# Another order of VectorE's and GpSimd's side work around the matmuls of a two-layer graph network

## The chip, the cores and the metric

The kernel runs on one core of one Trainium2 chip. The metric is the device time in microseconds, shown as the median of three runs. A profile of one further execution comes with it. In views of the profile PE is TensorE's matmul, PEld its weight load, DVE is VectorE, ACT is ScalarE, POOL is GpSimd, and SP is the queue that issues most DMAs.

## The reference

There are 32 independent inputs `x[b]` of 512 nodes by 512 features, all in float32, and one 512 by 512 adjacency matrix for all of them.

```python
# layer 0: attention over the graph, 8 heads of 64
q, k, v = x @ Wq + bq, x @ Wk + bk, x @ Wv + bv
w = softmax(q k^T / 8 + where(adj == 0, -1e9, 0))
x = layernorm(x + w v)
# layer 1: graph convolution
norm_adj = adj * deg**-0.5 (rows) * deg**-0.5 (columns)
x = layernorm(x + norm_adj @ (x @ weight) + bias)
```

## The kernel before, in words

The kernel goes over `b` = 0 to 31 in one long unrolled program. Almost every instruction goes through the helper class `InOrder` (line 45, which is why most rows of the profile name that line): it pins compute instructions to the order in which the program writes them, engine by engine. So the order in the text is the order on each engine.

**A pass and its two shares.** For each `b` there is a `stretch` over the first two pairs of attention-head pairs (`one`), then a list of matmul groups, then a `stretch` over the other two pairs (`two`), and a second list of matmul groups. I call the first list, with what runs beside it, the first share and the second list the second share. A `stretch` computes `scores` (tile `sc`, 32 matmul records on PE; VectorE subtracts the mask into `e`, ScalarE takes the exponential), then lets GpSimd sum the numerators (`acc`), and multiplies with the values (`av`, 32 records on PE).

- First share of `b`: keys and queries of the next input, `b + 1` (14 groups, tiles `kq`).
- Second share of `b`: the first product of the graph convolution of input `b - 1` (four groups, `first`), the values of input `b + 1` (`v`, eleven steps v[0] to v[10]), and the second product of the convolution (seven groups, `second`).

**Seven products for eight.** Keys, queries, values and the convolution are block products with seven multiplications instead of eight (`seven`). They need sums and differences of blocks of x transposed: `turn` transposes x into `XT[0..3]` on VectorE (two calls, `turn0` and `turn1`), and `combine` forms `XT[4..6]` and a new `XT[2]` on GpSimd (four operations). The values take one level more: v[0] to v[6] are `LEAF` groups on quarters of blocks, v[7] is an addition on GpSimd (`spread_last`), v[8] to v[10] are the `OUTER` groups. Their further combinations (`QUARTERS`, in `XT[7..10]`) are formed by `quarters`, four GpSimd operations. A group writes a PSUM bank and is then put (ScalarE) or added (VectorE) into its output. Groups named by the same letter in the table accumulate in the same bank, so the next of them may not write before the earlier one's put or add has read it. All three `OUTER` groups have one letter.

**Steps.** `play(main, beside)` issues the matmul groups of `main` one after the other, and behind group number n whatever `beside[n]` lists. I call n a step. In the second share for b = 1 to 29 the steps are: 0 to 3 `first`, 4 to 9 the leaf groups v[0] to v[5], 10 second[0], 11 the last leaf group v[6], 12 v[7], 13 v[8], 14 second[1], 15 v[9], 16 second[2], 17 v[10], 18 to 21 second[3] to second[6]. For b = 30 second[0] comes behind v[7] instead; for b = 0 there are only the eleven steps of `v`.

**What runs beside them.** `fold` (VectorE: one transposition and one reduction) finishes the softmax's sums; `inverse` is one small matmul (`folded`) and five VectorE operations; `scale` multiplies a row of the attention output by the inverse sums; `add` adds x (GpSimd); `measure`, `root`, `norm`, `low` and `lift` are the layer normalisation in pieces (`root` partly and `lift` wholly on GpSimd, `norm` on ScalarE, `low` on VectorE with the output `lo`); `grow` rescales on ScalarE; `bias_values` adds the values' bias row `bv_r` to one of four node rows of `V`.

DMAs of the pass go through SP: the head outputs' rearrangement (`yT<-yb`), two parts of the x after next, `wqv` in turn with the queries' and the values' weights (`swap`), and the outputs.

Of the kernel before, what the change touches and what calls it, by code (L numbers as in the profile page):

```python
# [50 lines left out]
def unshifted(  # L51
# [16 lines left out]
    NT = N // P  # L68
# [5 lines left out]
    tensor, vector, scalar, gpsimd = (InOrder(tc, e) for e in (nc.tensor, nc.vector, nc.scalar, nc.gpsimd))  # L74
# [24 lines left out]
    def each(f, *args):  # L99
        return [lambda a=a: f(*a) if isinstance(a, tuple) else f(a) for a in args]  # L100
# [22 lines left out]
    def load_x(b, j):  # L123
        if j == 1:
            X[b, j] = NUM[:, 7].rearrange("p k (n t r) -> p (k n) t r", t=DT, r=32)
        else:
            X[b, j] = acts.tile([P, 8, DT, 32], F32, name="x", bufs=1)
        for q in range(4):
            nc.sync.dma_start(
                X[b, j][32 * q : 32 * (q + 1)],  # L130
                x[b, ts(j, HALF), ts(q, P)].rearrange("(k s) (t r) -> s k t r", s=32, r=32),
            )

    def turn(b, j):
        vector.transpose(
            XT[:, 2 * j : 2 * j + 2].rearrange("p i u (k s) -> p (i u) k s", s=32),
            X.pop((b, j)).rearrange("p k t r -> p t k r"),
        )
# [26 lines left out]
    def combine(b, at):  # L165
        to, a, c = PARTS[at]
        engine = gpsimd if b else vector
        engine.tensor_tensor(XT[:, to], XT[:, a], XT[:, c], ALU.subtract)
# [15 lines left out]
    def load_residual(b):  # L184
        if b < LAST - 1:
            t = acts.tile([P, NT, D], F32, name="xr", tag="zT", bufs=1)
        else:
            t = wk[:, 3:].rearrange("p k u o -> p k (u o)")
        R[b] = [t[:, i, :] for i in range(NT)]
        for i in range(NT):  # L190
            nc.sync.dma_start(R[b][i], x[b, ts(i, P), :])
# [67 lines left out]
    def swap(k):  # L259
        nc.sync.dma_start(wqv, stored[k])  # L260
# [253 lines left out]
    def stretch(b, gs, gap=()):  # L514
        banks("attention")
        for g in gs:
            scores(b, g)
        for g in gs:
            accumulate(b, g)
        banks("products")  # L520
        for g in gs:
            av = bank([P, N], "av")
            values(b, g, av)
            unload_values(b, g, av)
            if g == gs[0]:
                run(gap)

    def fold(b, g):
        a = ACC.pop((b, g))[0]
        if g == ORDER[0]:  # L530
            SM[b] = small.tile([P, H, N // 32], F32, name="folded")
        vector.transpose(a.rearrange("p k n -> p (k n)"), a.rearrange("p k n -> p (k n)"))
        vector.tensor_reduce(
            SM[b][:, 2 * g : 2 * g + 2].rearrange("p k t -> p (k t)"),
            a.rearrange("p k (t s) -> p (k t) s", s=32), AX.X, ALU.add,
        )
# [306 lines left out]
    for b in range(B):  # L843
        one, two = ORDER[:2], ORDER[2:]
        f[b], c[b] = finish(b), convolve(b)
        ahead, back = f.get(b - 1), c.get(b - 2)
        if 1 < b < LAST:
            load_residual(b - 1)
        if b + 2 < B:
            load_x(b + 2, 0)  # L850
        if b == LAST:
            load_residual(b)
        stretch(b, one, back["measure"][:3] if back else ())

        def folds(gs):
            return [[lambda g=g, b=b: fold(b, g)] for g in gs]

        def turns(b=b + 2):
            if b >= B:
                return [], [], []  # L860
            return [lambda: turn(b, 0)], [lambda: turn(b, 1)], [lambda k=k: combine(b, k) for k in range(4)] + [quarters]

        fold0, fold1 = folds(one) if b < LAST else ([], [])
        rest = back["measure"][3:] + back["root"] if back else []
        store = back["store"] if back else []
        if b < LAST:
            k0, k1 = keys_and_queries(b + 1, 0), keys_and_queries(b + 1, 1)
            main = [p for pair in zip(k0, k1) for p in pair]
            if b == 0:
                exact = each(compare, *range(NT))  # L870
                weights = each(lambda k: weigh_part(w1, gpsimd, k), *range(4))
                beside = {
                    1: fold0, 2: [degrees], 3: weights[:1], 4: fold1, 5: weights[1:2] + exact[:1], 6: exact[1:2],
                    7: weights[2:3], 8: exact[2:3], 9: weights[3:], 10: exact[3:],
                }
            else:
                measure, norm, low = ahead["measure"], ahead["norm"], ahead["low"]
                scale = ahead["inverse"] + ahead["scale"] if b == 1 else []
                beside = {
                    0: rest + scale + ahead["add"], 1: store[:1] + fold0, 2: store[1:2], 3: store[2:3] + fold1,  # L880
                    4: store[3:] + measure[:2], 5: measure[2:] + ahead["root"], 7: norm[:1] + ahead["judge"],
                    8: norm[1:2] + low[:1], 9: norm[2:3] + low[1:2], 10: norm[3:] + low[2:3],
                    11: low[3:] + ahead["lift"],
                }
            play(main, beside)
        else:
            e = f[b]
            conv = c[b - 1]
            play(conv["first"], {
                0: rest + store[:1] + conv["parts"][:0], 1: store[1:2] + ahead["judge"] + conv["parts"][:1],  # L890
                2: store[2:] + e["sums0"],
                3: conv["parts"][1:] + e["inverse0"] + ahead["grow"],
            })

        if b < LAST:
            swap(1)
        stretch(b, two, f[b]["pairs"][0] + f[b]["pairs"][1] if b == LAST else ())

        fold0, fold1 = folds(two) if b < LAST else ([], [])
        turn0, turn1, combined = turns()  # L900
        if b + 2 < B:
            load_x(b + 2, 1)
        if b < LAST:
            end = f[b]
            v, bias_v = values_of(b + 1), each(bias_values, *((b + 1, n) for n in range(NT)))
            back_to_queries = [lambda: swap(0)] if b < LAST - 1 else []
            if b == 0:
                play(v, {
                    1: fold0, 4: fold1, 8: turn0, 9: turn1, 10: combined + back_to_queries + bias_v,
                })  # L910
            else:
                conv = c[b - 1]
                second = conv["second"]
                k = 6 if b < LAST - 1 else 8
                main = conv["first"] + v[:k] + second[:1] + v[k:9] + second[1:2] + v[9:10] + second[2:3] + v[10:] + second[3:]
                grow, parts, scale = ahead["grow"], conv["parts"], end["scale"]
                if b < LAST - 1:
                    bias_v = each(bias_values, *((b + 1, n, vector) for n in range(NT)))
                    beside = {
                        1: parts[:1] + fold0, 3: parts[1:], 5: fold1, 6: grow[:1], 8: grow[1:2], 9: grow[2:3] + end["inverse"],  # L920
                        10: grow[3:] + scale[:1], 11: scale[1:2], 13: turn0 + scale[2:3], 14: turn1 + scale[3:] + combined[:1],
                        15: combined[1:2], 17: combined[2:] + bias_v[:1] + back_to_queries, 18: bias_v[1:2],
                        19: bias_v[2:3], 20: bias_v[3:],
                    }
                else:
                    measure, norm, low = end["measure"], end["norm"], end["low"]
                    beside = {
                        0: [lambda: load_residual(LAST - 1)], 1: parts[:1] + fold0, 3: parts[1:], 5: fold1,
                        6: grow[:1], 8: grow[1:2], 9: end["inverse"], 10: grow[2:3] + scale[:2], 11: grow[3:] + scale[2:] + end["add"],
                        14: measure[:1], 15: measure[1:2], 16: measure[2:3],  # L930
                        17: measure[3:] + end["root"], 18: norm[:1] + bias_v, 19: norm[1:2] + low[:1], 20: norm[2:3] + low[1:2],
                        21: norm[3:] + low[2:] + end["lift"],
                    }
                play(main, beside)

# [5 lines left out]
    end, held, e = f[LAST], c[LAST - 1], c[LAST]  # L941
    pairs, halves, norm, low, block = (
        end["pairs"], end["halves"], end["norm"], end["low"], e["block"]
    )
# [302 lines left out]
```

## Time and profile before

| what | value |
|---|---|
| median of 3 runs | 2762.72 us (2760.16 to 2763.03) |
| profiled execution, own time | 2760.92 us |
| its span, first to last instruction | 2759.1 us |
| PE busy | 2715.4 us |
| VectorE busy | 2075.0 us |
| GpSimd busy | 1910.7 us |
| ScalarE busy | 1259.6 us |
| mean granted TensorE clock | 0.997 |

The page counts busy time of each engine over the whole span; the timeline gives the same instructions one by one; the waits say how long an engine idled and which engine's instruction ended that. From about 230 us on, one pass takes 84.47 us and repeats to the hundredth.

### The profile page before, as it was taken

Reading aid. Unit: us, or ns where it says so; the run is one execution under the profiler, and the core shown is the slowest. Engines: PE = TensorE matmul, PEld = TensorE weight load, DVE = VectorE, ACT = ScalarE, POOL = GpSimd, SP = SyncE. Lnnn points to the kernel's source line nnn. Section 1 sums busy time; section 2 is a strip of 40 time slices with the busy share of each in tenths; the row PEclk is TensorE's granted clock in tenths of the full one; section 3 lists DMA queues with packets and bytes.
Section 4 is the critical chain, followed back from the end, with each engine's and each line's share of the span. In section 5 each row is a group of like instructions: output and inputs, shape, how many; then the busy total and the mean of one; then the engine's idle time right before and its main releaser. Section 6 shows DMA issues by size and latency. Waiting matters only on the chain.

```text
span 2759.1 us, 36196 instructions
## 1 busy us (share of the span) xinstructions
PE 2715.4 (98%) x13284; PEld 1907.3 (69%) x13284; DVE 2075.0 (75%) x2925; ACT 1259.6 (46%) x1807; POOL 1910.7 (69%) x1219
## 2 busy tenths in 40 slices
PE   9899999999999999999999999999999999999997
PEld 6566776766767767667667676676676676766765
DVE  5777777778777777777787777777777877777777
ACT  3344444454434544444544445444445444454444
POOL 5667676676676676766766766767667677667675
PEclk9999999999999999999999999999999999999999
DMA  6223333333333233322333332333323333323321
GB/s 180 81 57 99 106 91 92 90 90 100 88 98 107 69 102 99 101 92 81 99 100 88 97 103 72 104 90 105 96 76 103 100 88 96 97 80 103 92 61 48
DMA packets 388185, 256.75 MB, mean 93 GB/s; under 512 B 278816, under 2 KB 346400, under 8 KB 379936
## 3 DMA queue, kind: packets, MB, share of 16 engines
q1 hardware_dynamic: 386848, 252.78, 30.5%
q8 instruction: 107, 1.75, 0.3%
q10 hardware_dynamic: 1152, 1.57, 0.2%
q14 instruction: 78, 0.64, 0.1%
HBM read 183.77 MB, written 37.22 MB: 80 GB/s over the span
## 4 chain that ended last, share of the span: by engine, by line
PE 90%; DVE 7%; issue 1%; POOL 1%; ACT 0%; DMA 0%; SPq 0%; DVEq 0%; POOLq 0%; ACTq 0%
PE mm L45 58%; PE av L45 16%; PE sc L45 16%; DVE xT L45 2%; DVE yT L45 2%; DVE v L45 2%; DVE y L45 1%; POOL xT L45 0%; DVE st L45 0%; DVE lo L45 0%; ACT yT L45 0%; ACT hi L45 0%; DVE e L45 0%; POOL y L45 0%; DMA xr<-in_x_dram 0%
## 5 line engine op out<-in xcount | busy, mean ns | idle before, releaser
L45 ACT ACTIVATE e<-e 128x1024 f32<-128x1024 f32 x512 | 541.4, 1057 | 614.8 <-DVE e L45 582.0
L45 DVE SCALAR_TENSOR_TENSOR e<-sc,maskT 128x1024 f32<-128x1024 f32 x512 | 584.8, 1213 | 103.1 <-PE sc L45 103.1
L45 POOL TENSOR_TENSOR acc<-acc,e 128x1024 f32<-128x1024 f32 x248 | 588.8, 2374 | 19.4
L45 POOL TENSOR_TENSOR xT<-xT 128x512 f32<-128x512 f32 x250 | 369.0, 1486 | 156.9 <-DVE xT L45 139.8
L45 PE MATMUL mm<-xT,wk 128*128 128x256 f32 x1792 | 463.5, 381 | 0.6 <-DVE kq L45 0.6
L45 PE MATMUL sc<-kq 64*128 64x512 f32 x2048 | 459.4, 597 | 1.8 <-DVE e L45 1.4
L45 PE MATMUL mm<-xT,wqv 128*128 128x256 f32 x1792 | 460.0, 379 | 0.0
L45 PE MATMUL av<-e,v 128*64 128x512 f32 x2048 | 455.4, 597 | 4.2 <-POOL v L45 4.0
L45 PEld LDWEIGHTS mm<-xT,wk 128*128 128x128 f32 x1792 | 337.3, 190 | 71.3 <-DVE mv L45 23.5
L45 POOL TENSOR_TENSOR acc<-e 128x1024 f32<-128x1024 f32 x126 | 297.3, 2360 | 118.5 <-ACT e L45 118.5
L45 PEld LDWEIGHTS mm<-xT,wqv 128*128 128x128 f32 x1792 | 340.4, 190 | 46.5 <-DVE wqv L45 0.2
L45 PEld LDWEIGHTS av<-e,v 128*64 128x64 f32 x2048 | 145.6, 137 | 306.6 <-issue 234.1
L45 PEld LDWEIGHTS sc<-kq 64*128 64x128 f32 x2048 | 191.7, 186 | 237.6 <-issue 182.6
L45 ACT ACTIVATE kq<-mm,bias 128x256 f32<-128x256 f32 x512 | 214.1, 472 | 295.7 <-PE mm L45 291.9
L45 PE MATMUL mm<-wqv,xT 128*128 128x128 f32 x1736 | 306.5, 322 | 15.2 <-DVE v L45 15.2
L45 POOL TENSOR_TENSOR yT<-yT,b_r 128x512 f32<-128x512 f32 x126 | 156.7, 1277 | 237.8 <-DVE lo L45 237.8
L45 DVE TENSOR_TENSOR v<-v,mm 128x512 f32<-128x512 f32 x221 | 148.6, 685 | 195.5 <-PE mm L45 195.3
L45 PEld LDWEIGHTS mm<-wqv,xT 128*128 128x128 f32 x1736 | 259.9, 191 | 49.3 <-DVE v L45 23.8
L45 DVE STREAM_TRANSPOSE yb<-av 128x512 f32<-128x512 f32 x127 | 91.0, 717 | 257.3 <-DMA yT<-yb 193.3
L45 PE MATMUL mm<-w,zT 128*128 128x256 f32 x992 | 229.5, 379 | 0.0
L45 PEld LDWEIGHTS mm<-w,zT 128*128 128x128 f32 x992 | 186.1, 190 | 24.8 <-issue 0.8
L45 PE MATMUL mm<-adjT,hi 128*128 128x512 f32 x512 | 201.6, 397 | 0.8 <-ACT e L45 0.8
(134 smaller groups left out, 3382.7 us busy)
## 6 DMA issues: line engine op xcount, KB each, us to landing
wqv<-wv_parts SPq DMA_DIRECT2D x31, 1792.0 KB, 7.5
wqv<-wq_parts SPq DMA_DIRECT2D x30, 1792.0 KB, 7.0
yT<-yb SPq DMA_DIRECT2D x508, 64.0 KB, 2.4
out_dram<-y SPq DMA_DIRECT2D x120, 256.0 KB, 2.0
xr<-in_x_dram SPq DMA_DIRECT2D x118, 256.0 KB, 3.3
x<-in_x_dram SPq DMA_DIRECT2D x124, 128.0 KB, 2.7
e<-in_x_dram SPq DMA_DIRECT2D x124, 128.0 KB, 2.6
wk<-in_x_dram SPq DMA_DIRECT2D x8, 256.0 KB, 2.7
```

What stands on the lines that cost most here:

```text
L45: return self.tc.keep_in_program_order(op(*args, **kwargs))
```

## The change

All of it lies in what stands beside the matmul groups.

- `quarters` for input `b + 2` are no longer formed behind `combine` in the second share of `b`, but in the first share of the next pass, behind `root` at step 5.
- In the second share, for b = 1 to 29: `inverse` moves from step 9 to step 7, `scale` from steps 10, 11, 13, 14 to 9, 10, 11, 14; the second transposition of x moves from step 14 to 15, and `combine` stands at steps 15 and 17. The bias of the values is added by GpSimd behind `combine` (four operations) and no longer by VectorE at steps 17 to 20.
- b = 0: `fold1` moves from step 4 to 5, and the bias comes behind two of the four `combine` operations.
- b = 30: `inverse` at step 7, the last row's `scale` at step 8, the others one step earlier, and everything behind them (`add`, `measure`, `root`, `norm`, `low`, `lift`) up to one step earlier.

```diff
-            return [lambda: turn(b, 0)], [lambda: turn(b, 1)], [lambda k=k: combine(b, k) for k in range(4)] + [quarters]
+            return [lambda: turn(b, 0)], [lambda: turn(b, 1)], [lambda k=k: combine(b, k) for k in range(4)]
...
-                    4: store[3:] + measure[:2], 5: measure[2:] + ahead["root"], 7: norm[:1] + ahead["judge"],
+                    4: store[3:] + measure[:2], 5: measure[2:] + ahead["root"] + [quarters], 7: norm[:1] + ahead["judge"],
...
-                    1: fold0, 4: fold1, 8: turn0, 9: turn1, 10: combined + back_to_queries + bias_v,
+                    1: fold0, 5: fold1, 8: turn0, 9: turn1 + combined[:2], 10: bias_v + combined[2:] + back_to_queries,
...
-                    bias_v = each(bias_values, *((b + 1, n, vector) for n in range(NT)))
                     beside = {
-                        1: parts[:1] + fold0, 3: parts[1:], 5: fold1, 6: grow[:1], 8: grow[1:2], 9: grow[2:3] + end["inverse"],
-                        10: grow[3:] + scale[:1], 11: scale[1:2], 13: turn0 + scale[2:3], 14: turn1 + scale[3:] + combined[:1],
-                        15: combined[1:2], 17: combined[2:] + bias_v[:1] + back_to_queries, 18: bias_v[1:2],
-                        19: bias_v[2:3], 20: bias_v[3:],
+                        1: parts[:1] + fold0, 3: parts[1:], 5: fold1, 6: grow[:1], 7: end["inverse"], 8: grow[1:2],
+                        9: grow[2:3] + scale[:1], 10: grow[3:] + scale[1:2], 11: scale[2:3], 13: turn0, 14: scale[3:],
+                        15: turn1 + combined[:2], 17: combined[2:] + back_to_queries + bias_v,
                     }
                 else:
...
-                        6: grow[:1], 8: grow[1:2], 9: end["inverse"], 10: grow[2:3] + scale[:2], 11: grow[3:] + scale[2:] + end["add"],
-                        14: measure[:1], 15: measure[1:2], 16: measure[2:3],
-                        17: measure[3:] + end["root"], 18: norm[:1] + bias_v, 19: norm[1:2] + low[:1], 20: norm[2:3] + low[1:2],
-                        21: norm[3:] + low[2:] + end["lift"],
+                        6: grow[:1], 7: end["inverse"], 8: grow[1:2] + scale[3:], 9: grow[2:3] + scale[:1], 10: grow[3:] + scale[1:3] + end["add"],
+                        14: measure[:2], 15: measure[2:3], 16: measure[3:] + end["root"],
+                        17: norm[:1] + bias_v, 18: norm[1:2] + low[:1], 19: norm[2:3] + low[1:2],
+                        20: norm[3:] + low[2:3], 21: low[3:] + end["lift"],
```

## The prediction

> **What bounds the kernel now.** I read the page's busy times, then PE's waits, then one period of the timeline engine by engine. The shared columns of the timeline are start, length, engine, line, operation, count, and in brackets the idle time ahead with its releaser.
>
> ```profile
> PE 2715.4 (98%) x13284; PEld 1907.3 (69%) x13284; DVE 2075.0 (75%) x2925; ACT 1259.6 (46%) x1807; POOL 1910.7 (69%) x1219
> PE 90%; DVE 7%; issue 1%; POOL 1%; ACT 0%; DMA 0%; SPq 0%; DVEq 0%; POOLq 0%; ACTq 0%
> ```
>
> The chain that ended last is 90% TensorE: only time in which PE issues nothing can be won. Its waits:
>
> ```profile
> PE mm L45 <- DVE v L45: 15.2, 33, 3.6
> PE av L45 <- POOL v L45: 4.0, 2, 3.8
> PE sc L45 <- DVE e L45: 1.4, 1, 1.4
> PE mm L45 <- DVE kq L45: 0.6, 1, 0.6
> ```
>
> 33 waits for VectorE's adds into `v`: the timeline has them as one in each of the 29 passes b = 1 to 29, three at b = 0, one at b = 30. In the pass at 1413 to 1497 us (period 84.47 us, the same from pass to pass):
>
> ```profile
> 1472.30 1.89 PE L45 MATMUL mm<-w,parts 128*128 128x256 f32 x8
> 1474.51 1.99 PE L45 MATMUL mm<-wqv,xT 128*128 128x256 f32 x8 [0.32 <-DVE v L45]
> 1476.34 1.89 PE L45 MATMUL mm<-w,zT 128*128 128x256 f32 x8
> ```
>
> Eight such matmuls issue in 1.73 us elsewhere in this stretch. From 1472.30 the next should start at 1474.03; it starts at 1474.51: **0.48 us** lost, and 0.10 more because these eight take 1.83. That group is the last of `OUTER` (v[10]). It accumulates into the bank that v[9] filled, so it waits for VectorE's add of v[9]. VectorE then:
>
> ```profile
> 1472.06 1.23 DVE L45 STREAM_TRANSPOSE xT<-e 128x1024 f32<-128x1024 f32 x1
> 1473.21 0.65 DVE L45 TENSOR_TENSOR yT<-yT,inv 128x512 f32<-128x512 f32 x1
> 1473.78 0.67 DVE L45 TENSOR_TENSOR v<-v,mm 128x512 f32<-128x512 f32 x1
> ```
>
> v[9]'s matmuls were issued by 1472.30, its add starts at 1473.78: it stands behind `turn1` and `scale[3]`. Two leaf groups are late too, 0.93 and 0.97 us for 0.89 (waiting for ScalarE's copy): 0.11. Sum **0.69 us per pass**.
>
> At b = 0 GpSimd is the late one:
>
> ```profile
> 114.19 4.17 PE L45 MATMUL mm<-wqv,xT 128*128 128x128 f32 x16 [3.56 <-DVE v L45]
> 134.95 1.08 PE L45 MATMUL av<-e,v 128*64 128x512 f32 x4 [3.84 <-POOL v L45]
> 136.18 7.84 PE L45 MATMUL av<-e,v 128*64 128x512 f32 x28 [0.15 <-POOL v L45]
> ```
>
> **What the skill says.** "SBUF — State Buffer", Who interferes with whom: a VectorE instruction with two SBUF inputs contends with a GpSimd instruction that reads SBUF. The trace agrees: the bias add on VectorE takes 691 ns alone and 1158 ns (median) beside GpSimd's `xT` work, and `lo` goes from 739 to 1362. "GPSIMD Engine Reference", Engine selection: two-input elementwise work about 2 times slower there; here 1277 ns against 691. "TensorE: Matmul & The Clock Gate", What's actually happening: after an idle window of about 3.4 us the clock falls to half. Seen here: the mean granted clock is 0.63 from 135 to 139 us, behind the wait of 3.84, and stays at 1.00 in periods with short waits. "Perfetto Trace Analysis", Identifying the Most-Contended Engine: matmul busy time misleads because matmuls are pipelined. So I measure losses by distances between starts.
>
> **The change, part by part, b = 1 to 29, second share** (times of the shown pass).
>
> 1. `inverse` moves from behind step 9 to behind step 7. PE's `folded` group (0.22) falls between leaf groups, which covers the 0.11 lost to ScalarE. It needs `fold1`, done at 1459.1, against 1462.4. VectorE's inverse takes 1.27 (1465.08 to 1466.35) and now stands ahead of two leaf adds: from 1462.87 (0.27 after PE, as other VectorE work follows PE) to 1464.14; the adds end at about 1464.8 and 1465.4. v[6] needs the second at 1466.1: 0.7 spare. Cost nothing; if the inverse is 0.3 later (bound), still 0.4 spare.
> 2. Scalings 0 to 2 go one or two steps earlier, into VectorE's gaps (idle 0.73 ahead of 1469.12). They end at about 1468.4, before v[8]'s add.
> 3. `turn0` stays. `scale[3]` is then done by about 1472.1, v[9]'s add runs 1472.6 to 1473.3, and `turn1` follows it. v[10] may start at 1474.03: 0.7 spare, so the stall goes. Late next: `turn1` ends at 1474.4 instead of 1473.3, and the second-layer add behind it at 1475.05; PE wants that bank again at 1477.5.
> 4. `combine` starts 1.0 later on GpSimd. Four at 1.27 to 1.49 end by about 1480.3; the third waits for v[10]'s reads, over by 1476. The four `quarters` leave (4 x 1.49), four bias adds come (4 x 1.28 to 1.46), ending at 1485.4 to 1486.2. v's adds they need are over at 1477.3. Behind them GpSimd's `acc` waits for ScalarE until 1488.0, and PE's `av` reads v from 1490.5: hidden, with 1.8 and 4.3 spare. The second queue, SP, keeps its order; its `wqv` load waits for v[10], not for the bias.
> 5. VectorE loses 116 bias adds, 120.9 us busy. Worth nothing: they ran between the last second-layer adds, which follow PE at its 1.73 us a group and need 0.68 of it; nothing behind them was late.
> 6. First share: `quarters` now run behind `root` on GpSimd, idle 7.72 us there (1427.7 to 1435.4); 4 x 1.49 fit. Their cost is contention with four `lo`: +0.4 to +0.6 each while quarters last, three of them, under 2 us, and with the gaps of 0.38 between `kq` adds `lo` ends some 0.3 to 1.2 later than 1435.3. VectorE's next work, `e`, starts at 1438.5: hidden. `lift` moves by as much; GpSimd has 1.67 idle behind it.
>
> So 29 x 0.69 = **20.0 us**. If all parts hold but the leaf term, 16.8.
>
> **b = 0.** v[6] waited for a leaf add standing behind `fold1`, which itself waited for GpSimd's `acc`. With `fold1` a step later the add follows two others at once, 110.96 to 111.64: v[6] starts near 111.7, not 114.19: 2.5. The following 16 matmuls took 4.0 us at reduced clock, 2.62 elsewhere: 1.4. The waits behind v[8] and v[9] (0.85 each) stay. Then `av`: `scores` start to `av` start is 10.98 us, 7.07 elsewhere: 3.9; `av` itself 9.0 for 7.02: 2.0. Bias rows now stand behind two `combine` rather than eight operations: `turn1` ends 0.8 before `scores`, so they end 6.7 to 7.6 behind its start, row by row, and `av` starts at 7.07 with the first row. The wait and the low clock go. Against that, at b = 1 VectorE is late already (`e` starts right behind the last `lo`), and the quarters beside `lo` are not hidden: 0 to 2.4, I take 1.1. Sum 2.5 + 1.4 + 3.9 + 2.0 - 1.1 = **8.7** (5 to 10).
>
> **b = 30.** Here v[6] follows the last leaf add directly; `inverse` and `scale[3]` put ahead of it cost about 0.9. In exchange `measure` and `root` come two microseconds earlier (`root` at about 2660 instead of 2661.5, though PE is later), so `lo` ends before `scores` need VectorE. That stretch takes 9.72 us (2666.17 to 2675.89), 7.07 undisturbed: 2.65. Net **1.8** (-1 to 2.7).
>
> Total 30.5. The profiled execution took 2760.92 us (span 2759.1 and 1.8 around it): 2730.4. The median of the runs shown is 1.8 us above it. I say **2731**.
>
> **Rivals.**
> - *The wait moves to v[6].* The inverse ahead of the leaf adds uses up its 0.7 us (a slower semaphore, `fold1` late). With 0.4 lost per pass the gain is 30.5 - 11.6: **2743**. For it: b = 0 and b = 30 show just this wait. Against: 0.7 to spare.
> - *b = 0 keeps its late GpSimd.* The bias still ends too late for `av` and the clock falls as before: 5.9 to 8.7 less, **2737 to 2740**. For it: GpSimd still has eight operations ahead of `acc` there. Against: the order, which puts six of them ahead of the last bias row instead of twelve.
> - *GpSimd becomes the bound in the second share: slower.* It decides when bias adds end later than `av`'s first read, 4.3 us after my estimate. Each us beyond costs 29 us in all: with 2 us past, 58 are lost against 30.5 won: **2789**. For it: four adds of 1.3 to 1.5 in front of `acc`, which also feeds `fold0` of the next share. Against: the quarters that leave cost as much, and GpSimd has 2.09 idle ahead of `acc` now.
> - *The change doesn't do what it says.* Each engine's instructions in the built program stand in the written order, since all but DMA issues are pinned; little room for that.
>
> **Numbers.** Forecast 0.62 (its own range 2724 to 2738), wait at v[6] 0.18, b = 0 unimproved 0.08, slower 0.08, no change within 0.2% (5.5 us, about what a measurement of this kernel can tell) 0.04. Faster 0.88. Low end: with the 0.10 us ahead of `sc` in each pass (1437.34 instead of 1437.24) also gone and the upper bounds, 23 + 10 + 2.7 give 2725; 0.1% of scatter, as the runs show, makes 2722. High end: takes in the wait at v[6] with a weak start, 2748.
>
> **What would show it.** Right: PE's wait on DVE `v` drops from 33 to about 4, period 83.8 us, no PE wait on POOL `v`, `lo` up to 1.2 us beside quarters, POOL `v<-v,bv_r` x128. Wrong: a period still near 84.4 with a wait at the `wqv,xT` group behind `folded` (v[6]), or PE `av` waiting for POOL.

## The result, and the profile after

The changed kernel takes **2731.85 us** (median of five runs, 2730.91 to 2733.34), the kernel before 2760.16 (five runs, 2759.36 to 2763.03): ratio **0.9895**, 95% interval 0.988 to 0.9909, so about 1.05% faster. The profiled execution took 2731.85 us with a span of 2730.0.

From the page: busy time and share of each engine, and the chain that ended last by engine.

```profile
PE 2700.8 (99%) x13284; PEld 1907.7 (70%) x13284; DVE 2023.7 (74%) x2809; ACT 1260.5 (46%) x1807; POOL 2026.7 (74%) x1335
PE 97%; DVE 2%; ACT 0%; DMA 0%; issue 0%; POOL 0%; SPq 0%; POOLq 0%; DVEq 0%; ACTq 0%
```

The instruction counts show the bias adds crossing over: 116 fewer on VectorE, 116 more on GpSimd. VectorE's share of the last chain fell from 7% to 2%. PE's waits (total, times, longest):

```profile
PE mm L45 <- DVE v L45: 4.5, 4, 1.6
PE mm L45 <- DVE kq L45: 2.3, 1, 2.3
```

The 29 regular waits for `v` are gone, and `av` no longer waits for GpSimd. Two waits have grown: that for `kq` at b = 1, from 0.6 to 2.3, and that for `v` at b = 30, from 0.65 to 1.58. In the pass from 1395 us on, the timeline of PE around v[10] (the middle line), then that of VectorE before it:

```profile
1452.88 1.89 PE L45 MATMUL mm<-w,parts 128*128 128x256 f32 x8
1454.60 1.89 PE L45 MATMUL mm<-wqv,xT 128*128 128x256 f32 x8
1456.33 1.89 PE L45 MATMUL mm<-w,zT 128*128 128x256 f32 x8
```

```profile
1453.15 0.69 DVE L45 TENSOR_TENSOR v<-v,mm 128x512 f32<-128x512 f32 x1 [0.44 <-PE mm L45]
1453.75 1.24 DVE L45 STREAM_TRANSPOSE xT<-e 128x1024 f32<-128x1024 f32 x1
```

The starts on PE are 1.72 and 1.73 apart. VectorE now even waits 0.44 for v[9], adds it, and transposes afterwards. One pass takes 83.78 us instead of 84.47.

Where the 29.1 us between the two spans came from, by distances between the same instructions in both profiles:

| stretch | before | after | difference |
|---|---|---|---|
| start of the second share, b = 0 | 104.90 | 103.97 | -0.93 |
| from there to `scores` | 19.07 | 15.39 | -3.68 |
| `scores` and `av` | 19.98 | 14.22 | -5.76 |
| from there to the second share of b = 1 | 40.50 | 41.86 | +1.36 |
| 29 second and 29 first shares, to the second `scores` of b = 30 | 2435.42 | 2415.45 | -19.97 |
| from there to the last pass's first product | 63.03 | 62.35 | -0.68 |
| the rest | 76.20 | 76.76 | +0.56 |

The first row is in front of anything the change touches, and the last row is mostly the end behind the last product. The five rows between them add up to 28.7 us.

### The profile page after: what moved, and what is told of

It reads as the page before. It is cut to its first block, busy times and chain, and to the rows that moved or that the text cites. A ratio compares the mean times of both kernels' runs of the same rounds, so it can differ in the third digit from the quotient of the medians.

```text
span 2730.0 us, 36290 instructions
## 1 busy us (share of the span) xinstructions
PE 2700.8 (99%) x13284; PEld 1907.7 (70%) x13284; DVE 2023.7 (74%) x2809; ACT 1260.5 (46%) x1807; POOL 2026.7 (74%) x1335
## 3 DMA queue, kind: packets, MB, share of 16 engines
q8 instruction: 107, 1.75, 0.3%
## 4 chain that ended last, share of the span: by engine, by line
PE 97%; DVE 2%; ACT 0%; DMA 0%; issue 0%; POOL 0%; SPq 0%; POOLq 0%; DVEq 0%; ACTq 0%
PE mm L45 64%; PE sc L45 17%; PE av L45 16%; DVE st L45 0%; DVE yT L45 0%; DVE xT L45 0%; DVE lo L45 0%; DVE v L45 0%; DVE kq L45 0%; POOL y L45 0%; DMA xr<-in_x_dram 0%; SPq L509 0%; DVE e L45 0%; DVE mv L45 0%; DVE folded L45 0%
## 5 line engine op out<-in xcount | busy, mean ns | idle before, releaser
L45 POOL TENSOR_TENSOR xT<-xT 128x512 f32<-128x512 f32 x250 | 342.8, 1385 | 176.4 <-DVE xT L45 168.9
```

The source lines that it names most:

```text
L45: return self.tc.keep_in_program_order(op(*args, **kwargs))
```

## The experiments

In brief, the median of each kernel beside that of the kernel before, measured next to it:

| run | us | before | difference |
|---|---|---|---|
| VectorE's order alone, b = 1 to 29 | 2757.22 | 2761.24 | -4.0 |
| GpSimd half alone, b = 1 to 29 | 2761.29 | 2761.24 | 0.0 |
| both halves, b = 1 to 29 | 2741.98 | 2761.71 | -19.7 |
| transposition alone | 2761.58 | 2761.24 | +0.3 |
| transposition and GpSimd half | 2743.55 | 2761.71 | -18.2 |
| b = 0 alone | 2752.44 | 2761.24 | -8.8 |
| changed, bias back on VectorE | 2746.34 | 2761.28 | -14.9 |
| changed, quarters back | 2732.07 | 2761.28 | -29.2 |
| changed, quarters twice | 2857.9 | 2761.28 | +96.6 |
| changed, two scalings early | 2755.41 | 2761.28 | -5.9 |
| changed, edges mended | 2732.62 | 2760.67 | -28.1 |
| changed again | 2731.96 | 2760.67 | -28.7 |

My theory was the prediction's: VectorE's order carries the 20 us of the passes, and what goes to GpSimd is hidden either way. The rival was that VectorE's load, that is the bias adds, matters.

### VectorE's order alone

```diff
                     bias_v = each(bias_values, *((b + 1, n, vector) for n in range(NT)))
-                        10: grow[3:] + scale[:1], 11: scale[1:2], 13: turn0 + scale[2:3], 14: turn1 + scale[3:] + combined[:1],
-                        15: combined[1:2], 17: combined[2:] + bias_v[:1] + back_to_queries, 18: bias_v[1:2],
+                        ... 7: end["inverse"], 9: grow[2:3] + scale[:1], 10: grow[3:] + scale[1:2], 11: scale[2:3], 13: turn0, 14: scale[3:],
+                        15: turn1 + combined[:2], 17: combined[2:] + bias_v[:1] + back_to_queries, 18: bias_v[1:2],
```

> The kernel before, with VectorE's new order alone in the second share of b = 1 to 29 (inverse at step 7, scalings at 9, 10, 11 and 14, second transposition at 15). The bias stays on VectorE, the quarters stay in the second share, b = 0 and b = 30 stay. My theory: the order of VectorE's work alone removes the stall ahead of v[10] and the two late leaf groups, 0.69 us in each of 29 passes: about 20 us faster than before, 2740, and PE waits on DVE v 4 times instead of 33. Rival, that relieving VectorE of the bias or GpSimd of the quarters is what frees it: about 2760, no change.

Measured: ratio 0.9984 (0.9978 to 0.9991), 4.0 us faster. Both sides missed: the waits for `v` fell to 4 as the theory has it, but PE got 28 waits of another kind, and a pass takes 84.35 us, only 0.12 less than before. PE's waits:

```profile
PE mm L45 <- DVE y L45: 7.9, 28, 0.3
PE mm L45 <- DVE v L45: 6.0, 4, 3.6
```

### The GpSimd half alone

```diff
-            ... [lambda k=k: combine(b, k) for k in range(4)] + [quarters]
+            ... [lambda k=k: combine(b, k) for k in range(4)]
-                    5: measure[2:] + ahead["root"], 7: norm[:1] + ahead["judge"],
+                    5: measure[2:] + ahead["root"] + ([quarters] if b > 1 else []), 7: norm[:1] + ahead["judge"],
-                    bias_v = each(bias_values, *((b + 1, n, vector) for n in range(NT)))
-                        15: combined[1:2], 17: combined[2:] + bias_v[:1] + back_to_queries, 18: bias_v[1:2], ...
+                        15: combined[1:2], 17: combined[2:] + back_to_queries + bias_v,
```

> The kernel before, with the other half alone for b = 1 to 29: quarters formed in the next first share, bias added by GpSimd, VectorE's order as before (b = 0 and b = 30 as before). My theory: no change within 0.2%, 2757 to 2763, the wait ahead of v[10] still there 29 times; the 116 bias adds and the moved quarters are hidden. Rival, that VectorE's load counts: up to 20 us faster, 2740.

Measured: ratio 1.0001 (0.9992 to 1.0009). No change, as the theory says; PE still waits for `v` 33 times. This alone would have supported "the bias is worth nothing".

### The transposition alone

```diff
-                        14: turn1 + scale[3:] + combined[:1], 15: combined[1:2],
+                        14: scale[3:], 15: turn1 + combined[:2],
```

> The kernel before, with one move for b = 1 to 29: the second transposition of x (with the combine that follows it) from behind step 14 to behind step 15, thus behind VectorE's add of v[9]. My theory: the stall of 0.48 and the 0.10 behind it go, the two late leaf groups (0.11) stay: 29 x 0.58 = 17 us faster than before, 2743. Rival, that the earlier scalings are needed too: less than 5 us faster, 2756 or more.

Measured: ratio 1.0001 (0.9992 to 1.0009). The move of which I expected 17 us gave none. Its timeline, PE first (v[10], second[5], second[6]), shows v[10] on time and a stall four groups later:

```profile
545.32 1.89 PE L45 MATMUL mm<-wqv,xT 128*128 128x256 f32 x8
...
550.50 1.89 PE L45 MATMUL mm<-w,zT 128*128 128x256 f32 x8
552.74 1.97 PE L45 MATMUL mm<-w,zT 128*128 128x256 f32 x8 [0.35 <-DVE y L45]
```

552.74 is 2.24 behind 550.50 where 1.73 is due: 0.51 lost, and 0.1 behind it, as much as was won ahead. VectorE in that stretch:

```profile
548.57 1.75 DVE L45 TENSOR_TENSOR v<-v,bv_r 128x512 f32<-128x512 f32 x1
550.24 0.67 DVE L45 TENSOR_TENSOR y<-y,mm 128x512 f32<-128x512 f32 x1
550.84 1.16 DVE L45 TENSOR_TENSOR v<-v,bv_r 128x512 f32<-128x512 f32 x1
551.92 0.68 DVE L45 TENSOR_TENSOR y<-y,mm 128x512 f32<-128x512 f32 x1
```

second[6] accumulates into the bank of second[4], whose add into `y` is the last line, ended at 552.60. It stands behind two bias adds beside GpSimd's `xT` work. The same place in the kernel before, VectorE's timeline:

```profile
1477.86 0.69 DVE L45 TENSOR_TENSOR v<-v,bv_r 128x512 f32<-128x512 f32 x1
...
1480.15 0.67 DVE L45 TENSOR_TENSOR y<-y,mm 128x512 f32<-128x512 f32 x1
```

There the add ends at 1480.82 and PE wants the bank at 1481.53: 0.7 spare. The first bias add has used it up: it takes 1.75 instead of 0.69, 1.06 more (less the 0.71 spare, and with the 0.15 from the add's end to the matmul, that is the 0.51). GpSimd's timeline shows why, first of the kernel before, then of this one; each line is one subtraction of `combine`:

```profile
1477.94 1.74 POOL L45 TENSOR_TENSOR xT<-xT 128x512 f32<-128x512 f32 x1
```

```profile
548.50 1.27 POOL L45 TENSOR_TENSOR xT<-xT 128x512 f32<-128x512 f32 x1
```

In the kernel before, the bias add starts first, 0.08 ahead of the subtraction, and it is the subtraction that takes long (1.74 for 1.27). Here the subtraction starts first, 0.07 ahead of the bias add, and the add ends 0.55 behind its end (550.32 against 549.77). The order has turned because `combine` follows the transposition: it now starts 0.60 behind v[10] (545.92 against 545.32), where it started 1.08 ahead of it (1473.43 against 1474.51). That PE is 0.58 earlier doesn't matter here: the bias add stands behind v[10]'s own adds, and comes as long behind v[10] as before (3.25 us for 3.35).

One pass of this kernel serves as a control. At b = 2 `combine` starts 0.3 later still (why, I have not traced), so that the bias add meets only the last 0.28 of a subtraction. The lines are VectorE's, GpSimd's and PE's (second[5] and second[6] in one):

```profile
295.60 0.82 DVE L45 TENSOR_TENSOR v<-v,bv_r 128x512 f32<-128x512 f32 x1
294.61 1.27 POOL L45 TENSOR_TENSOR xT<-xT 128x512 f32<-128x512 f32 x1
297.53 3.62 PE L45 MATMUL mm<-w,zT 128*128 128x256 f32 x16
```

v[10] is on time there too and the bias is on VectorE, yet PE doesn't wait: this is why there are 28 waits for `y` and not 29. With VectorE's order alone it is again the pass b = 2 (first bias add 0.75) that has no such wait.

### The first pass alone

```diff
-                    1: fold0, 4: fold1, 8: turn0, 9: turn1, 10: combined + back_to_queries + bias_v,
+                    1: fold0, 5: fold1, 8: turn0, 9: turn1 + combined[:2], 10: bias_v + combined[2:] + back_to_queries,
```

with that pass's quarters behind `root` of b = 1, all others as before.

> The kernel before, with the change at b = 0 alone: fold1 at step 5, bias behind two of the four combine operations, the quarters of that pass in the first share of b = 1. My theory: 3.7 won between v and scores, 5.8 at av, 1.4 lost at b = 1 where quarters slow VectorE: 8 us faster than before, 2752, and no PE wait on POOL v. Rival, that the lost clock comes back anyway or GpSimd stays late: 0 to 3 us.

Measured: ratio 0.9968 (0.9956 to 0.998), 8.8 us faster; no PE wait on POOL `v`, and the wait for `kq` of 2.3 at b = 1. The part of the prediction on b = 0 stands on its own.

### The changed kernel with the bias back on VectorE

```diff
-                        15: turn1 + combined[:2], 17: combined[2:] + back_to_queries + bias_v,
+                        15: turn1 + combined[:2], 17: combined[2:] + bias_v[:1] + back_to_queries, 18: bias_v[1:2],
+                        19: bias_v[2:3], 20: bias_v[3:],
```

> The changed kernel, with the bias of the values back on VectorE for b = 1 to 29 (steps 17 to 20, between the last second-layer adds); the quarters stay in the first share. My theory: 116 adds of about 0.7 to 1.2 us stand in gaps of that stretch: no change, 2732 within 3 us. Rival, that VectorE's load counts or its first e is late: 5 to 20 us slower.

Measured: ratio 0.9946 (0.9932 to 0.996), 2746.34 us, some 14 us slower than the changed kernel. The theory falls for this part; the rival's size holds, and the wait for `y` is back 28 times. PE's waits:

```profile
PE mm L45 <- DVE y L45: 7.8, 28, 0.3
```

By distances a wait costs 0.51 (its eight matmuls start 0.43 late, and 0.08 follows); 28 x 0.51 = 14.3. Here the subtraction starts 0.13 ahead of the first bias add, which takes 1.67: 0.08 less than with the transposition alone, and the stall is 0.08 shorter too. The one pass without the wait is b = 2 again, where that add takes 0.77; it lasts 83.8 us, no longer than in the changed kernel. So the load of four bias adds alone is not what costs, but how they meet GpSimd.

My new theory was: two stalls stand one behind the other on PE, v[10] behind the transposition and second[6] behind the bias adds, and the first hands VectorE the time that hides the second. Taking away one alone then shows nothing. The next two runs test that.

### Both halves, and the transposition with the GpSimd half

The first is the order of the first experiment and the edit of the second together; the other has only the transposition's move and the edit of the second.

> The kernel before, with both halves for b = 1 to 29 (VectorE's order, and quarters and bias as in the changed kernel), b = 0 and b = 30 as before. The order alone gave 4 us, the GpSimd half alone nothing. Theory now: two stalls stand behind one another on PE, v[10] behind the transposition and second[6] behind the bias adds, and the first gave VectorE the time that hid the second; with both gone the whole 20 us come: 2741. Rival, that the halves only add: 2757.

> The kernel before, with the second transposition behind step 15 as the one move on VectorE, plus the GpSimd half (quarters and bias) for b = 1 to 29; inverse and scalings where they were before. The transposition alone gave nothing. Theory: these two are what the pass needs, 0.58 of the 0.69: 17 us faster than before, 2744, 3 us slower than both halves. Rival, that inverse and scalings carry the gain: 2757 or more.

Measured: both halves 0.9929 (0.9915 to 0.9942), 19.7 us faster; transposition and GpSimd half 0.9938 (0.9925 to 0.9952), 18.2 us faster. PE's waits of the first, with no line for `y`:

```profile
PE mm L45 <- DVE v L45: 5.9, 4, 3.6
```

-4 and 0 alone, -20 together: the halves don't add, as the new theory says. Its reason is wrong, though. The stall at v[10] did not hide the second one: at b = 2 it is gone and no second one comes. The move of the transposition makes the second stall, by letting GpSimd start ahead of the bias add, and the move of the bias takes that add away. The earlier inverse and scalings give some 1.5 us more, and the intervals of the two runs overlap; but in the profiles the pass takes 83.79 with them and 83.89 without, 0.10 less, close to the 0.11 of the prediction.

### How much cover GpSimd had

In the changed kernel the bias comes first on GpSimd, then `acc`, with time to spare. GpSimd's timeline (`av` starts at 1470.40):

```profile
1455.13 5.19 POOL L45 TENSOR_TENSOR xT<-xT 128x512 f32<-128x512 f32 x4 [5.04 <-DVE xT L45]
1460.29 4.94 POOL L45 TENSOR_TENSOR v<-v,bv_r 128x512 f32<-128x512 f32 x4
1468.03 2.36 POOL L45 TENSOR_TENSOR acc<-e 128x1024 f32<-128x1024 f32 x1 [2.80 <-ACT e L45]
```

The first edit puts the quarters back in front of the bias from b = 1 on, the second forms them there twice.

```diff
-                        15: turn1 + combined[:2], 17: combined[2:] + back_to_queries + bias_v,
+                        15: turn1 + combined[:2], 17: combined[2:] + [quarters] + back_to_queries + bias_v,
```

> The changed kernel, with the quarters put back into the second share (from b = 1 on), between combine and the bias on GpSimd: the bias then ends 5 to 6 us later. My theory: GpSimd's bias ended at about 1465.2 in the changed kernel's pass where av starts at 1470.4; with four more operations the rows end at 1466.7 to 1471.3, and av reads the last row only some 2.6 us behind its start, so it is hidden, just: 2732 within 3 us. Rival, that GpSimd is the bound there: 1 us or more in each pass, 2760 or more.

> As the run with the quarters back in the second share, but each of the four formed twice (the second time the same values over the first), so that the bias ends another 5 to 6 us later, at about 1477 against av's start at 1470.4. My theory: now GpSimd sets av's start: 2.5 to 4 us in each of 29 passes, 2805 to 2850, and PE waits on POOL v in each pass. Rival, that there is still cover: 2735.

Measured: once 0.9895 (0.988 to 0.991), the same as the changed kernel; twice 1.0351 (1.0332 to 1.0369), 126 us slower than the changed kernel. With the quarters once, GpSimd's and then PE's timeline read

```profile
543.40 4.98 POOL L45 TENSOR_TENSOR v<-v,bv_r 128x512 f32<-128x512 f32 x4
```

```profile
548.35 7.09 PE L45 MATMUL av<-e,v 128*64 128x512 f32 x32
```

The last bias row ends just as `av` starts, which costs nothing: the quarters' move in itself is worth nothing. With eight quarters, PE's timeline:

```profile
558.51 7.14 PE L45 MATMUL sc<-kq 64*128 64x512 f32 x32
567.00 1.08 PE L45 MATMUL av<-e,v 128*64 128x512 f32 x4 [1.34 <-POOL v L45]
568.23 1.08 PE L45 MATMUL av<-e,v 128*64 128x512 f32 x4 [0.15 <-POOL v L45]
...
590.75 1.13 PE L45 MATMUL mm<-xT,wk 128*128 128x256 f32 x4 [1.54 <-ACT kq L45]
```

`av` comes at the pace of the bias rows; from `scores` to the next `kq` group it is 16.63 us (575.14 less 558.51) instead of 14.09. Another 1.8 is lost when PE later waits for ScalarE's `kq` (1.7, and 0.1 behind it). Together 4.34 per pass, and 29 x 4.34 = 126. ScalarE is late because its `kq` stands behind its `y`, which waits for the second part of `root` on GpSimd (`add`, ended at 586.27). ScalarE's timeline:

```profile
586.30 0.82 ACT L45 ACTIVATE y<-y,add,rstd 128x512 f32<-128x512 f32 x1 [6.57 <-POOL add L45]
```

### The spare time of v[6]

```diff
-                        ... 7: end["inverse"], 8: grow[1:2], 9: grow[2:3] + scale[:1], 10: grow[3:] + scale[1:2],
+                        ... 7: end["inverse"] + scale[:2], 8: grow[1:2], 9: grow[2:3], 10: grow[3:],
```

> The changed kernel, with scalings 0 and 1 at step 7, right behind the inverse, thus ahead of two leaf adds on VectorE for b = 1 to 29 (1.2 us more in front of them). This measures the spare time that the prediction gave to v[6], 0.7 us. My theory: v[6] is 0.57 us late in each pass and 0.1 more for the interrupted weights: 16 to 20 us slower than the changed kernel, 2748 to 2752. Rival, that the spare time is larger than that: 2732; that it is near nothing: 35 us slower, 2767.

Measured: 2755.41 us, ratio to before 0.9981 (0.9973 to 0.9989), 23 us slower than the changed kernel, 0.8 per pass where I expected 0.67. In the changed kernel the second leaf add ends 0.72 before v[6] starts (1446.08 against 1446.80); the two scalings delay it by 1.32 (442.00 to 443.32), and the start follows the add by 0.15. The first line is the group before v[6], cut by the window; the second begins with v[6]. PE's timeline of this kernel:

```profile
442.70 1.46 PE L45 MATMUL mm<-w,zT 128*128 128x256 f32 x6
444.75 2.86 PE L45 MATMUL mm<-wqv,xT 128*128 128x128 f32 x16 [0.59 <-DVE v L45]
```

So the spare time was as read: for the prediction's first rival, VectorE would have had to be some 0.7 us later there than it is.

### The edges mended

The last two lines of the edit are given in words.

```diff
-                    1: fold0, 5: fold1, 8: turn0, 9: turn1 + combined[:2], 10: bias_v + ...
+                    1: fold0, 5: fold1, 8: end["inverse"] + turn0, 9: end["scale"][3:] + turn1 + combined[:2], 10: bias_v + ...
-                scale = ahead["inverse"] + ahead["scale"] if b == 1 else []
+                scale = ahead["scale"][:3] if b == 1 else []
+                    (b == 1: ahead["judge"] at step 11 behind low and lift, not at 7)
+                    (b == 30: end["inverse"] and scale[3:] at step 9, not at 7 and 8)
```

> The changed kernel, with its two edges mended. b = 0 and 1: the inverse and one scaling of b = 0 move into the second share of b = 0, where VectorE idles, and judge at b = 1 stands behind the last lo. b = 30: the inverse and the last row's scaling stand behind the last leaf add. My theory: the wait for kq at b = 1 (2.3 us in the changed kernel) goes to below 0.5 and v[6] at b = 30 starts about 0.9 earlier: 2.5 to 3 us faster than the changed kernel, 2729. Rival, that the time is given back later in these passes: 2731 to 2732.

> The changed kernel itself, on the same chip and beside the same runs of before as the mended one, for comparison: 2732, a ratio of 0.9895.

Measured: mended 0.9899 (0.9883 to 0.9916), the changed kernel again 0.9894 (0.9878 to 0.9911). No gain; the rival holds. The wait for `kq` went, but in the same pass PE now waits for VectorE's `e`, since `judge` has only moved in front of it; PE's timeline of the mended kernel at b = 1 and b = 30:

```profile
163.57 4.52 PE L45 MATMUL sc<-kq 64*128 64x512 f32 x16 [1.15 <-DVE e L45]
...
2619.09 1.13 PE L45 MATMUL mm<-wqv,xT 128*128 128x128 f32 x8 [0.65 <-DVE v L45]
...
2626.16 1.99 PE L45 MATMUL mm<-wqv,xT 128*128 128x256 f32 x8 [0.76 <-DVE v L45]
```

At b = 30 v[6] comes 0.9 earlier and v[9] pays it back. I have found no version that beats the changed kernel.

## Why the prediction was right or wrong, point by point

The forecast was 2731, the measured median 2731.85. The sum was right, with some luck; one step of its reasoning was not. The parts forecast 30.5 us and won 28.7: b = 30 gave 1.1 less and b = 0 0.6 less. That 2731 is still less than 1 us off is because the profiled execution began 0.9 earlier for reasons outside the change, and because the forecast was rounded up by 0.6.

- **The leaf groups, v[6] and v[10]** (parts 1 to 3): right. The waits fell from 33 to 4, the pass went from 84.47 to 83.78, and 29 x 0.69 came as 19.97.
- **"Worth nothing"** (part 5): wrong. I priced a bias add by the fact that the second-layer adds "need 0.68" of the 1.73 us per group. A group has to hold both: from one add's start to the next it is 0.60 for the `y` add and 1.08 for a bias add beside GpSimd, 1.68 of 1.73. And I misread the 691 ns as a bias add "alone". All 29 adds of that length ran beside GpSimd too and had only started 0.08 ahead of its subtraction. Part 3 moves `combine` along with the transposition and turns that order, so the first bias add would take 1.67 to 1.75. I followed the delay only to the next add behind `turn1`, and took the length of the later ones from the old profile. Without moving the bias to GpSimd 14 us of the gain would have been lost. The change moves it anyway, so the sum didn't suffer; by my reasons that was luck.
- **GpSimd's cover** (part 4): right, and larger than priced: bias rows end at 1465.2, 5.2 before `av`, where I had 4.3. The slower rival's mechanism is real, but its point lies at least 5 us of GpSimd work further than the change goes, as the run with the quarters once shows.
- **Quarters beside `lo`** (part 6): right. `lo` went from 746 to 1036 ns in the median, and GpSimd's `lift` still ends before `acc`. In the passes from b = 2 on nothing of it reached PE.
- **b = 0**: -3.68 for 3.9, -5.76 for 5.9, +1.36 for 1.1. The last is the term whose mechanism I had wrong: it is not `lo` alone. VectorE's small `judge` operation meets the quarters too (1.14 us for 0.19), and PE waits for the first of the four `kq` adds behind it. VectorE also comes there 0.64 later behind the start of that share; 0.5 of this is its four scalings, which take 6.65 us for 6.14. VectorE's timeline at b = 1:

```profile
154.79 0.17 DVE L45 TENSOR_SCALAR low<-inv 128x32 f32<-128x32 f32 x1
155.00 1.14 DVE L45 SCALAR_TENSOR_TENSOR low<-inv,low 128x32 f32<-128x32 f32 x1
156.18 0.19 DVE L45 TENSOR_REDUCE fine<-low 128x1 f32<-128x32 f32 x1
```

- **b = 30**: 0.68 for 1.8. The loss at v[6] came as forecast (1.58 waited instead of 0.65). Of the 2.65 expected at `scores` 1.92 came: the stretch takes 7.80 us, not 7.07, as `lo` beside GpSimd's bias still ends after `scores` have begun. Another 0.34 went where nothing was forecast: second[6] waits for a second-layer add that stands behind a `lo` of 1.38 us.
- **The clock at b = 0**: right. The granted clock stays at 1.00 from 119 to 134 us, with no PE wait over 1.2 us in that share; this agrees with what the Trainium skill says under "TensorE: Matmul & The Clock Gate", What's actually happening, on idle windows of about 3.4 us.

## What to carry to other kernels

The length of an instruction in a trace holds for the order in which it met its neighbours there. The bias add of 0.69 us had started just ahead of a GpSimd instruction; behind one it takes up to 1.75. So where a move shifts the work of one of two engines that delay each other, ask for each later deadline which of the two now starts first, and price the instruction with the rest of the other's in front of it. One move can take away a stall and make another a few groups later; then each part of a change alone can show little or nothing, although together they give everything. A helper's load is judged by its pitch between two deadlines, all its instructions of that stretch added up, not by each one's own length.

## What the runs showed of the hardware that I had not expected

- In the cases measured, VectorE and GpSimd delay each other by the rest of an instruction, and the one that starts second waits. Every bias add of the kernel before that starts during one of GpSimd's `xT` subtractions (87 of 116), and every `lo` of the changed kernel that does so (90), ends 0.55 us behind the end of that subtraction. So the loss is not in proportion to the VectorE instruction. A 128x32 operation took 1.14 us instead of 0.19 (`low<-inv,low`, above; it ends at 156.14, the subtraction beside it at 156.09), while most 128x512 `lo` grow by only 0.43 (0.74 to 1.17), because 0.6 us of the subtraction is left when they start.
- 0.08 us decide about 1 us: the same bias add took 0.69 in all 29 passes of the kernel before, where it starts that much ahead of the subtraction, and 1.75 where it starts 0.07 behind it.
- An operation with a single input from SBUF is held up as well: in the changed kernel `judge`'s first one (`low<-inv`, 128x32) takes about 1.2 us instead of 0.17 in most passes, and ends 0.04 behind the subtraction.
